# A graph attention kernel: Q by edge in SBUF two batches ahead, E in two PSUM banks one batch ahead, block sums in Q's bank, and gathers tied at every second batch

## The chip, the cores and the metric

The kernel runs on one core of one Trainium2 chip. Time is device time in microseconds (us) of one execution; the kernel before has a median of 2043.54 us over ten runs (2042.44 to 2047.0). The engines are TensorE (PE in the profile, PEld for its weight loads), VectorE (DVE), ScalarE (ACT), GpSimd (POOL) and SyncE (SP, whose queue issues most transfers).

## The reference

One layer of attention over a graph with 6250 nodes and 206250 directed edges, eight heads of 16 columns, followed by a residual and a layer norm:

```
Qh, Kh, Vh = h @ WQ, h @ WK, h @ WV            # 6250 x 128 each
Eh = edge_attr @ WE                            # 206250 x 128
score = exp(clip(sum_d(Kh[src] * Qh[dst] * Eh) / 4, -5, 5))     # per edge and head
msg = Vh[src] * score
h_out = segment_sum(msg, dst) / (segment_sum(score, dst) + 1e-6)
x = layernorm(x + h_out)
```

Edges come sorted by dst. src is random, so the rows of K and V must be gathered.

## The kernel before, in words

**Tiles and batches.** The edges are cut into 1612 tiles of 128. `cut_batches` joins four tiles into a batch of 512 edges (the last five batches are smaller), which gives 406 batches. The main loop at L481 runs once for each batch b, and four times more to drain.

**Tables.** At the start `table` (L226) computes K and V of every node and stores them to device memory as `kv` (1 KB a row). `q_rows` (L256) computes Q of 128 nodes, splits it into three bf16 parts and stores them as `qs`; `load_q` (L269) loads a window of 42 nodes (126 rows of parts) for eight tiles.

**Gathers.** `gather(b)` (L308) issues, for each tile of a batch, one indirect DMA on POOL (L315), which fetches 128 rows by `src` into a buffer of the pool "gather" with GB = 15 buffers. The first 12 batches (XB) fetch rows of x instead, and `project` (L326) makes K and V out of them on PE while the table is still being written. From batch 16 (LOCK) on, the first gather of every batch carries a manual dependency (L318 to L323), the tie: it waits for Q's matmul of batch b - lag(b). `lag` falls from 12 to STEP = 1 as b grows and stays at 1 from batch 60 on.

**The work of a batch**, spread over four iterations:

- `stage_0` (called two batches ahead, AHEAD = 2), on DVE: the one-hot matrix of edges by node, `onehot` (L343, f32), and its transposed form by Q's rows, `onehotT` (L347, bf16).
- `stage_a` (iteration b), on PE: Q by edge, `qps` (L357), copied to SBUF by ACT as `qT` (L359, two buffers); then E, `eps` (L361), which stays in PSUM.
- `pairs` (iteration b), on DVE: `eq` = qT times eps (L368).
- `turn` (iteration b + 1), on PE: four transposes of eq into `pps` (L376).
- `stage_b` (iteration b + 2), on DVE: `kq` = gathered K times pps (L382), the sum by head `sc` (L385), the clip (L388).
- `weigh` (iteration b + 2), on ACT: the two exponentials (L394, L396).
- `messages` (iteration b + 3), on DVE: `msg` = gathered V times weight (L423), the last use of the gather's buffer.
- `stage_c` (iteration b + 3), on PE: `agg` (L441), one-hot times messages, summed in PSUM for eleven tiles, copied by ACT (L454). `finish` (L407) joins such sums for two blocks of 128 nodes (`finps`), and `layernorm` follows in single steps that `fill` puts between other DVE instructions.

**Order of the work.** Each engine runs its instructions in the order in which they were issued. From iteration 12 on (`manual_schedule`, L483) that is the order written in the loop; before, Tile's scheduler may change it. In iteration b, PE runs turn(b-1), Q(b), E(b), then agg(b-3). DVE runs stage_b(b-2), messages(b-3), onehot and onehotT of b+2, then pairs(b). Other one-time work on DVE stands early: `from_window(1)` at batch 14 (L152 to L165), `relative` at batch 20 (L178), `count_inside` at batch 60 (L191 to L201).

**PSUM.** Eight banks: one for E (`psE`), one for Q (`psQ`), two for pps (`psP`), one (`psT`, tag "oT") for row blocks, projections' transposes, finishing sums and the count, two for agg (`psA`) and one (`psX`) that is always in use. The tables and the projections borrow from the first three through `pair_bank` (L218).

Of the kernel before, what the change touches and what calls it, by code (L numbers as in the profile page):

```python
# [8 lines left out]
F32 = mybir.dt.float32  # L9
I32 = mybir.dt.int32  # L10
BF16 = mybir.dt.bfloat16
# [13 lines left out]
MW = D + H  # L25
B = 4
CH = 8
GB = 15
XB = 12
LOCK = XB + 4  # L30
STEP = 1
TAIL = 8
HEAD = 132
NG = (NT + G - 1) // G
AHEAD = 2
EB = 6
SLAG = 2
WT = 8
# [42 lines left out]
def edge_attention(ctx: ExitStack, tc: tile.TileContext, x, xT, srcT, dstT, dstB, dst0, bnd, lo, eaT,  # L81
# [30 lines left out]
    with ExitStack() as fast:  # L112
# [78 lines left out]
        def count_inside():  # L191

            W = 4 * 2 * D
            for a in range(0, NT, W):
                e = min(NT, a + W)
                cl = wp.tile([P, W], F32, name="cl", tag="kvst", bufs=2)[:, :e - a]
                count(P, cl, rel[:, a:e], P - 1)
            nc.vector.tensor_reduce(cn[:, :1], cn, axis=AX.X, op=ALU.add)
            pc = psT.tile([1, 1], F32, name="pc", tag="oT")
            nc.tensor.matmul(pc, cn[:, :1], ones, start=True, stop=True)  # L200
            nc.vector.tensor_copy(cnt_i, pc)  # L201

# [1 line left out]
        ep = fast.enter_context(tc.tile_pool(name="edges", bufs=EB))  # L204
        wp = fast.enter_context(tc.tile_pool(name="work", bufs=3))
        sp = fast.enter_context(tc.tile_pool(name="sums", bufs=7))
        psE = fast.enter_context(tc.tile_pool(name="psE", bufs=1, space=bass.MemoryType.PSUM))
        psQ = fast.enter_context(tc.tile_pool(name="psQ", bufs=1, space=bass.MemoryType.PSUM))
        psP = fast.enter_context(tc.tile_pool(name="psP", bufs=2, space=bass.MemoryType.PSUM))
        psT = fast.enter_context(tc.tile_pool(name="psT", bufs=1, space=bass.MemoryType.PSUM))  # L210
        psA = fast.enter_context(tc.tile_pool(name="psA", bufs=2, space=bass.MemoryType.PSUM))
        psX = fast.enter_context(tc.tile_pool(name="psX", bufs=1, space=bass.MemoryType.PSUM))

# [3 lines left out]

        def pair_bank(i, name, shape):  # L218

            pool, tag = ((psE, "eps"), (psP, "pps"), (psQ, "qps"), (psP, "pps"))[i % 4]  # L220
            return pool.tile(shape, F32, name=name, tag=tag)


# [31 lines left out]

        def q_rows(q):  # L256
            n = min(P, N - q * P)
            ps = psT.tile([P, D], F32, name="qrows", tag="oT")
            nc.tensor.matmul(ps[:n], xT_sb[:, LEFT + q * P:LEFT + q * P + n], wq_sb, start=True, stop=True)
            st = wp.tile([P, QP, D], BF16, name="qst", bufs=1)  # L260
            r1 = wp.tile([P, D], F32, name="qr1", bufs=1)
            nc.scalar.copy(st[:n, 0, :], ps[:n])
            nc.vector.tensor_tensor(r1[:n], ps[:n], st[:n, 0, :], op=ALU.subtract)
            nc.scalar.copy(st[:n, 1, :], r1[:n])
            nc.vector.tensor_tensor(st[:n, 2, :], r1[:n], st[:n, 1, :], op=ALU.subtract)
            nc.sync.dma_start(qs[q * P * QP:(q * P + n) * QP].rearrange("(p s) f -> p s f", s=QP), st[:n])
            built.append(q)
# [17 lines left out]
            nc.sync.dma_start(rels[c][:, :n], relD.rearrange("j e -> (j e)")[None, c * RC * P:c * RC * P + n]  # L285
                              .to_broadcast([QROWS, n]))

        chunks, aggs, sums, pair_sums, st8, expanded = {}, {}, {}, {}, {}, {}

        def load_chunk(c):  # L290
            if c in chunks or c * CH >= NT:
# [16 lines left out]
        def gather(b, made=None):  # L308
            rows, f = (x, D) if b < XB else (kv, 2 * D)
            g = gp.tile([P, B, 2 * D], F32, name="kvrows")  # L310
            for i, t in enumerate(batches[b]):
                k = min(P, (E - t * P + 63) // 64 * 64)
                if k < P:
                    nc.vector.memset(g[k:, i, :], 0.0)
                ins = nc.gpsimd.indirect_dma_start(  # L315
                    out=g[:k, i, :f], out_offset=None, in_=rows,
                    in_offset=bass.IndirectOffsetOnAxis(ap=src_col(t)[:k], axis=0))
                if i == 0 and b >= LOCK:  # L318
                    made = expanded[b - lag(b)]
                if i == 0 and made is not None:  # L320
                    tc.add_manual_dep(ins.ins, made.ins.name,
                                      mybir.DependencyInfo(mybir.DependencyClass.Sync, mybir.DependencyReason.DATA),
                                      reason="gathers keep to TensorE's pace")  # L323
            return g

        def project(g, n):  # L326

            pt = psT.tile([P, B, P], F32, name="xtps", tag="oT")
            for i in range(n):
                nc.tensor.transpose(pt[:, i, :], g[:, i, :D], ident)  # L330
            xgT = wp.tile([P, B, P], F32, name="xgT", tag="kq", bufs=2)
            nc.scalar.copy(xgT[:, :n], pt[:, :n])
            for i in range(0, n, 2):
                k = min(2, n - i)
                pk = pair_bank(i // 2, "kvps", [P, 2, 2 * D])
                for j in range(k):
                    nc.tensor.matmul(pk[:, j, :], xgT[:, i + j, :], wkv_sb, start=True, stop=True)
                nc.scalar.copy(g[:, i:i + k, :], pk[:, :k, :])  # L338

        def stage_0(b):  # L340
            t0, n = batches[b][0], len(batches[b])
            oh = wp.tile([P, B, P], F32, name="onehot", bufs=AHEAD + 5)
            nc.vector.tensor_tensor(oh[:, :n], iota_p[:, None, :].to_broadcast([P, n, P]),  # L343
                                    rel[:, t0:t0 + n, None].to_broadcast([P, n, P]), op=ALU.is_equal)
            ohT = wp.tile([QROWS, B * P], BF16, name="onehotT", bufs=AHEAD + 2)
            e0 = t0 % RC * P
            nc.vector.tensor_scalar(ohT[:, :n * P], rels[t0 // RC][:, e0:e0 + n * P], node[:QROWS], None,  # L347
                                    op0=ALU.is_equal)
            st8[b] = oh, ohT

        def stage_a(b, g):
            t0, n = batches[b][0], len(batches[b])
            if b < XB:
                project(g, n)
            oh, ohT = st8.pop(b)
            pq = psQ.tile([P, B * P], F32, name="qps")
            expanded[b] = nc.tensor.matmul(pq[:, :n * P], loaded[t0 // WT], ohT[:, :n * P], start=True, stop=True)  # L357
            qT = wp.tile([P, B * P], F32, name="qT", bufs=2)
            nc.scalar.copy(qT[:, :n * P], pq[:, :n * P])  # L359
            pe = psE.tile([P, B * P], F32, name="eps")  # L360
            nc.tensor.matmul(pe[:, :n * P], we_sb, ea_tiles(t0, n), start=True, stop=True)  # L361
            st8[b] = [n, g, oh, pe, qT]

        def pairs(b):

            n, g, oh, pe, qT = st8[b]
            eq = wp.tile([P, B * P], F32, name="eq", bufs=2)
            nc.vector.tensor_tensor(eq[:, :n * P], qT[:, :n * P], pe[:, :n * P], op=ALU.mult)  # L368
            st8[b] = [n, g, oh, eq]

        def turn(b):

# [34 lines left out]
        def finish(j):  # L407

            q = 2 * j
            ps = psT.tile([P, 2, MW], F32, name="finps", tag="oT")  # L410
            for r in range(3):
                nc.tensor.matmul(ps, shift[:, P - OFF[r]:2 * P - OFF[r]], pair_sums[j][:, r], start=r == 0, stop=False)  # L412
            rest = [(i, (q + i + d, r), d * P + OFF[r]) for i in range(2) for d, r in ((-1, 2), (1, 0))]
            rest = [x for x in rest if x[1] in sums]
            for n, (i, k, s) in enumerate(rest):
                nc.tensor.matmul(ps[:, i], shift[:, P - s:2 * P - s], sums[k], start=False, stop=n == len(rest) - 1)
            fin = sp.tile([P, 2, MW], F32, name="fin", bufs=2)
            nc.scalar.copy(fin, ps)
            pending.append(layernorm(nc, sp, fin, xbs.pop(q), out, q, 2, stores))
# [55 lines left out]
        def fill():  # L475

            if norms and next(norms[0], None) is None:
                norms.pop(0)

        held = []  # L480
        for b in range(nbat + 4):  # L481
            if b >= XB and not manual:
# [5 lines left out]
            if b < nbat:  # L488
# [7 lines left out]
                    relative(C0, NT)  # L496
                if b == 14:
                    from_window(1)
                if b == 0:
                    for i in range(AHEAD):  # L500
                        stage_0(i)
                if b > 0:
                    turn(b - 1)
                stage_a(b, g)
            elif b == nbat:
                turn(b - 1)
            norms.extend(pending)
            pending.clear()
            for j in ready:
# [4 lines left out]
            if 0 <= b - 3 < nbat:  # L514
                messages(b - 3)
            fill()
            if b + AHEAD < nbat:
                stage_0(b + AHEAD)
            if b < nbat:
                pairs(b)  # L520
            if 0 <= b - 2 < nbat:
                weigh(b - 2)
            if 0 <= b - 3 < nbat:
                stage_c(b - 3)
            fill()
            if b < nbat:
                while len(built) < q_built(min(NJ - 1, batches[b][0] // WT + QLOOK + 2)):
                    q_rows(len(built))
# [162 lines left out]
```

## Time and profile before

| what | value |
|---|---|
| median of ten runs | 2043.54 us (2042.44 to 2047.0) |
| the profiled execution, its own time | 2044.03 us |
| its span in the trace | 2042.2 us |
| granted clock of TensorE, mean | 0.878 |
| busy: PE / DVE / ACT / POOL | 1431.8 / 1565.1 / 473.3 / 1533.8 us |
| gathers on POOL | 48 of x rows and 1564 of K and V rows, mean 951 ns |
| first and last gather's start | 3.60 and 2026.36 us |
| kq (L382): time that DVE waited for gathered rows | 348.7 us, 162 times |

The rest comes from one profiled execution. A row of a group gives line, engine and operation, what is written from what, the count, then busy time and mean ns, then the engine's idle time just before such instructions and what ended most of it. A row of the timeline gives start, duration, engine, line and operation, and in brackets the idle time before it. A row of the waits gives the total, the number of times and the longest, in us. Registers, semaphores and the issuing of a transfer on a queue are not counted as busy.

### The profile page before, as it was taken

Reading aid. Unit: us, or ns where it says so; the run is one execution under the profiler, and the core shown is the slowest. Engines: PE = TensorE matmul, PEld = TensorE weight load, DVE = VectorE, ACT = ScalarE, POOL = GpSimd, SP = SyncE. Lnnn points to the kernel's source line nnn. Section 1 sums busy time; section 2 is a strip of 40 time slices with the busy share of each in tenths; the row PEclk is TensorE's granted clock in tenths of the full one; section 3 lists DMA queues with packets and bytes.
Section 4 is the critical chain, followed back from the end, with each engine's and each line's share of the span. In section 5 each row is a group of like instructions: output and inputs, shape, how many; then the busy total and the mean of one; then the engine's idle time right before and its main releaser. Section 6 shows DMA issues by size and latency. Waiting matters only on the chain.

```text
span 2042.2 us, 24333 instructions
## 1 busy us (share of the span) xinstructions
PE 1431.8 (70%) x6736; PEld 992.2 (49%) x6736; DVE 1565.1 (77%) x3542; ACT 473.3 (23%) x1548; POOL 1533.8 (75%) x1619
## 2 busy tenths in 40 slices
PE   6977876776776667666767667776766676666765
PEld 4655554454544445444454444444544444444544
DVE  3689998777777778677787777776877777777776
ACT  2422222221222222222222222221222222222221
POOL 7777777777777777777777777777777777777775
PEclk9989998888889888889788888888888888888888
DMA  9777766656666676666665676667565666666652
GB/s 300 225 230 204 221 200 207 192 173 217 186 198 183 187 209 175 203 174 200 201 188 175 197 204 198 185 186 214 171 203 172 201 208 180 195 178 203 202 170 82
DMA packets 177711, 398.12 MB, mean 195 GB/s; under 512 B 60988, under 2 KB 86758, under 8 KB 177568
## 3 DMA queue, kind: packets, MB, share of 16 engines
q0 software_dynamic: 76592, 208.18, 34.8%
q1 hardware_dynamic: 99836, 187.38, 29.6%
q8 instruction: 56, 0.92, 0.2%
q10 hardware_dynamic: 1140, 0.93, 0.2%
q14 instruction: 87, 0.71, 0.1%
HBM read 381.54 MB, written 14.81 MB: 194 GB/s over the span
## 4 chain that ended last, share of the span: by engine, by line
DMA 33%; DVE 28%; POOL 17%; issue 12%; PE 8%; ACT 1%; DVEq 0%; SPq 0%; POOLq 0%; ACTq 0%
DMA kvrows<-kv,src 32%; POOL kvrows L315 17%; DVE kq L382 7%; DVE sc L385 7%; DVE msg L423 3%; DVE eq L368 3%; DVE onehot L343 3%; PE agg L441 3%; PE eps L361 2%; DVE onehotT L347 2%; DVE sc L388 1%; PE pps L376 1%; DMA kv<-kvst 1%; PE qps L357 1%; PE finps L412 0%
## 5 line engine op out<-in xcount | busy, mean ns | idle before, releaser
L315 POOL DMA_INDIRECT kvrows<-kv,src x1564 | 1487.2, 951 | 476.5 <-issue 362.0
L441 PE MATMUL agg<-msg,onehot 128*128 128x136 f32 x3224 | 530.9, 314 | 512.8 <-DVE msg L423 410.5
L441 PEld LDWEIGHTS agg<-msg,onehot 128*128 128x128 f32 x3224 | 470.5, 215 | 833.1 <-issue 666.6
L382 DVE TENSOR_TENSOR kq<-kvrows,pps 128x512 f32<-128x512 f32 x406 | 275.6, 679 | 351.2 <-DMA kvrows<-kv,src 348.7
L361 PE MATMUL eps<-ea,we_sb 128*128 128x512 f32 (+1 forms) x812 | 478.5, 674 | 0.7 <-ACT kvrows L338 0.7
L359 ACT COPY qT<-qps 128x512 f32<-128x512 f32 x406 | 236.3, 582 | 544.5 <-PE qps L357 542.8
L376 PE MATMUL pps<-shift,eq 128*128 128x128 f32 x1612 | 302.2, 317 | 62.9 <-DVE eq L368 59.5
L368 DVE TENSOR_TENSOR eq<-qT,eps 128x512 f32<-128x512 f32 x406 | 273.3, 673 | 20.7 <-PE eps L361 16.7
L385 DVE TENSOR_REDUCE sc<-kq 128x32 f32<-128x512 f32 x406 | 276.1, 680 | 8.9
L423 DVE TENSOR_TENSOR msg<-kvrows,bank 128x512 f32<-128x512 f32 x406 | 274.4, 676 | 5.5 <-ACT bank L394 5.4
L343 DVE TENSOR_TENSOR onehot<-bank,dst_sb 128x512 f32<-128x512 f32 x406 | 274.9, 678 | 0.0
L394 ACT ACTIVATE bank<-sc 128x32 f32<-128x32 f32 x406 | 81.8, 201 | 823.8 <-DVE onehot L343 812.3
L376 PEld LDWEIGHTS pps<-shift,eq 128*128 128x128 f32 x1612 | 208.0, 160 | 120.8 <-DVE eq L368 114.8
L361 PEld LDWEIGHTS eps<-ea,we_sb 128*128 128x128 f32 x812 | 180.5, 224 | 29.8 <-ACT kvrows L338 3.7
L357 PE MATMUL qps<-onehotT,qw 126*128 126x512 bf16 x406 | 177.9, 438 | 0.7 <-ACT qT L359 0.7
L347 DVE TENSOR_SCALAR onehotT<-relb,node 126x512 bf16<-126x512 bf16 x406 | 154.7, 382 | 6.0 <-DMA relb<-relD 5.2
L388 DVE TENSOR_SCALAR sc<-sc 128x32 f32<-128x32 f32 x406 | 90.1, 222 | 9.0
L396 ACT ACTIVATE msg<-sc 128x32 f32<-128x32 f32 x406 | 86.5, 213 | 0.2
L315 POOL DMA_INDIRECT kvrows<-x,src x48 | 45.6, 951 | 16.4 <-issue 12.2
L454 ACT COPY sum<-agg 128x136 f32<-128x136 f32 x146 | 38.6, 264 | 33.1 <-PE agg L441 31.4
L357 PEld LDWEIGHTS <-qw 126*128 126x128 bf16 x406 | 45.1, 111 | 1.1 <-issue 1.0
L412 PE MATMUL finps<-sum,shift 128*128 128x272 f32 x144 | 37.4, 397 | 0.0
(69 smaller groups left out, 465.5 us busy)
## 6 DMA issues: line engine op xcount, KB each, us to landing
ea<-eaT SPq DMA_DIRECT2D x201, 512.0 KB
relb<-relD SPq DMA_DIRECT2D x100, 504.0 KB
kvrows<-kv,src POOLq DMA_INDIRECT x1564
qw<-qs SPq DMA_DIRECT2D x202, 31.5 KB
kv<-kvst SPq DMA_DIRECT2D x12, 512.0 KB
qs<-qst SPq DMA_DIRECT2D x48, 96.0 KB
xb<-x SPq DMA_DIRECT2D x24, 128.0 KB
out<-h SPq DMA_DIRECT2D x24, 128.0 KB
```

The lines of the kernel that those rows point to most:

```text
L315: ins = nc.gpsimd.indirect_dma_start(out=g[:k, i, :f], out_offset=None, in_=rows, in_offset=bass.IndirectOffsetOnAxis(ap=src_col(t)[:k], a ...
L343: nc.vector.tensor_tensor(oh[:, :n], iota_p[:, None, :].to_broadcast([P, n, P]), rel[:, t0:t0 + n, None].to_broadcast([P, n, P]), op=ALU.i ...
L347: nc.vector.tensor_scalar(ohT[:, :n * P], rels[t0 // RC][:, e0:e0 + n * P], node[:QROWS], None, op0=ALU.is_equal)
L357: expanded[b] = nc.tensor.matmul(pq[:, :n * P], loaded[t0 // WT], ohT[:, :n * P], start=True, stop=True)
L359: nc.scalar.copy(qT[:, :n * P], pq[:, :n * P])
L361: nc.tensor.matmul(pe[:, :n * P], we_sb, ea_tiles(t0, n), start=True, stop=True)
L368: nc.vector.tensor_tensor(eq[:, :n * P], qT[:, :n * P], pe[:, :n * P], op=ALU.mult)
L376: nc.tensor.transpose(pp[:, i, :], eq[:, i * P:i * P + P], ident)
L382: nc.vector.tensor_tensor(t1[:, :n], g[:, :n, :D], pp[:, :n], op=ALU.mult)
L385: nc.vector.tensor_reduce(sc[:, :n], t1[:, :n].rearrange("p b (h d) -> p b h d", h=H), axis=AX.X, op=ALU.add)
L423: nc.vector.tensor_tensor(m[:, :n, :D].rearrange("p b (h d) -> p b h d", h=H), g[:, :n, D:].rearrange("p b (h d) -> p b h d", h=H), exp_p[ ...
L441: nc.tensor.matmul(aggs[k], oh[:, i, :], m[:, i, :], start=first and not final, stop=last)
```

## The change

Three constants change: GB from 15 to 14, STEP from 1 to 0, and AHEAD is replaced by QA = 2 and EA = 1. `stage_0` and `stage_a` are cut into four functions.

- Q's matmul and its copy to SBUF (`expand_q`) run two batches ahead, at the end of the iteration, behind agg; `qT` gets four buffers, and `onehotT` three.
- E's matmul (`expand_e`) runs one batch ahead, into one of two banks, at Q's former place behind the transposes of `turn`.
- `onehotT` is still built two batches ahead, now ahead of the other; `onehot` is built in iteration b itself, just before `pairs`.
- Row blocks, projections' transposes, finishing sums and the count go to Q's bank; the bank `psT` is gone, and its place is E's second.
- The tie names E's matmul of batch b - lag(b), where lag now falls to 0 (at batch 64), and only even batches have it.
- Before the loop, onehotT and Q of batches 0 and 1 and E of batch 0 are issued.

```diff
-GB = 15
+GB = 14
-STEP = 1
+STEP = 0
-AHEAD = 2
+QA = 2
+EA = 1
...
-            pc = psT.tile([1, 1], F32, name="pc", tag="oT")
+            pc = psQ.tile([1, 1], F32, name="pc", tag="qps")
...
-        psE = fast.enter_context(tc.tile_pool(name="psE", bufs=1, space=bass.MemoryType.PSUM))
+        psE = fast.enter_context(tc.tile_pool(name="psE", bufs=2, space=bass.MemoryType.PSUM))
-        psT = fast.enter_context(tc.tile_pool(name="psT", bufs=1, space=bass.MemoryType.PSUM))
...
-            pool, tag = ((psE, "eps"), (psP, "pps"), (psQ, "qps"), (psP, "pps"))[i % 4]
+            pool, tag = ((psE, "eps"), (psP, "pps"))[i % 2]
...
-                if i == 0 and b >= LOCK:
+                if i == 0 and b >= LOCK and b % 2 == 0:
                     made = expanded[b - lag(b)]
...
-            pt = psT.tile([P, B, P], F32, name="xtps", tag="oT")
+            pt = psQ.tile([P, B, P], F32, name="xtps", tag="qps")
...
+        def one_hot(b):
+            t0, n = batches[b][0], len(batches[b])
+            hot[b] = wp.tile([P, B, P], F32, name="onehot", bufs=6)
+            nc.vector.tensor_tensor(hot[b][:, :n], iota_p[:, None, :].to_broadcast([P, n, P]),
                                     rel[:, t0:t0 + n, None].to_broadcast([P, n, P]), op=ALU.is_equal)
+        def one_hot_rows(b):
+            hotT[b] = wp.tile([QROWS, B * P], BF16, name="onehotT", bufs=3)
...
+        def expand_q(b):
+            pq = psQ.tile([P, B * P], F32, name="qps")
+            nc.tensor.matmul(pq[:, :n * P], loaded[t0 // WT], hotT.pop(b)[:, :n * P], start=True, stop=True)
+            qTs[b] = wp.tile([P, B * P], F32, name="qT", bufs=QA + 2)
+            nc.scalar.copy(qTs[b][:, :n * P], pq[:, :n * P])
+        def expand_e(b):
+            pes[b] = psE.tile([P, B * P], F32, name="eps")
+            expanded[b] = nc.tensor.matmul(pes[b][:, :n * P], we_sb, ea_tiles(t0, n), start=True, stop=True)
+        def pairs(b, g):
+            eq = wp.tile([P, B * P], F32, name="eq", bufs=3)
+            nc.vector.tensor_tensor(eq[:, :n * P], qTs.pop(b)[:, :n * P], pes.pop(b)[:, :n * P], op=ALU.mult)
...
+        for b in range(QA):
+            one_hot_rows(b)
+            expand_q(b)
+        for b in range(EA):
+            expand_e(b)
...
-                if b > 0:
-                    turn(b - 1)
-                stage_a(b, g)
-            elif b == nbat:
+            if 0 < b <= nbat:
                 turn(b - 1)
+            if b < nbat and b < XB:
+                project(g, len(batches[b]))
+            if b + EA < nbat:
+                expand_e(b + EA)
...
-            if b + AHEAD < nbat:
-                stage_0(b + AHEAD)
+            if b + QA < nbat:
+                one_hot_rows(b + QA)
             if b < nbat:
-                pairs(b)
+                one_hot(b)
+                pairs(b, g)
...
             fill()
+            if b + QA < nbat:
+                expand_q(b + QA)
```

## The prediction

> **What bounds the kernel now.** I read the busy shares first, then who waits for whom, then single instructions in order of time. The busy shares alone mislead: VectorE (DVE) is busiest, and the chain that ended last is put down to DMA and DVE.
>
> ```profile
> PE 1431.8 (70%) x6736; PEld 992.2 (49%) x6736; DVE 1565.1 (77%) x3542; ACT 473.3 (23%) x1548; POOL 1533.8 (75%) x1619
> POOL 7777777777777777777777777777777777777775
> DMA 33%; DVE 28%; POOL 17%; issue 12%; PE 8%; ACT 1%; DVEq 0%; SPq 0%; POOLq 0%; ACTq 0%
> L315 POOL DMA_INDIRECT kvrows<-kv,src x1564 | 1487.2, 951 | 476.5 <-issue 362.0
> L382 DVE TENSOR_TENSOR kq<-kvrows,pps 128x512 f32<-128x512 f32 x406 | 275.6, 679 | 351.2 <-DMA kvrows<-kv,src 348.7
> ```
>
> POOL stands at 7 tenths in every slice but the last: that evenness is the clue. Its idle time before gathers, 476.5 us over 1564, is 0.305 us each. The waits of POOL show that no pause before a gather is longer, whatever is named as releaser:
>
> ```profile
> POOL kvrows L315 <- issue: 374.1, 1228, 0.3
> POOL kvrows L315 <- DVE sc L388: 19.2, 63, 0.3
> POOL kvrows L315 <- DVE kq L382: 14.0, 46, 0.3
> POOL kvrows L315 <- PE eps L361: 13.7, 45, 0.3
> ```
>
> In all 1612 rows of POOL's timeline the pause is 0.29 to 0.32 us, on first gathers of a batch (which carry the tie) and on the others alike (the first of all, which waited for its indices, apart). So neither tie nor buffer ever held POOL: it issues a gather each 0.95 + 0.30 = 1.25 us, without a hole, from 3.60 to 2026.36 us. 1611 steps of 1.2505 are 2014.6; the other 8.8 us are gathers that took longer (69 of them above 0.965 us). After the last gather's start come 15.8 us of tail to the span's 2042.2. DVE's 348.7 us for kq are DVE waiting for POOL's rows: it does a batch in some 3.6 us when rows are there (kq to kq, shortest 3.58), POOL gives one each 5.0.
>
> **What the change must do to matter.** Time moves only if POOL stops, a gather gets longer, or the tail moves. I take the edits by these three.
>
> *Ties.* A gather's first piece waits now for Q's matmul of batch b-1; then for E's matmul of batch b, at even b only. Removing half the ties frees 0 us, as tied gathers show the same 0.30. Both matmuls stand in iteration b-1 behind the same transposes, so the new one ends later by E instead of Q: 1.02 less 0.38 at full clock, up to 1.9 less 0.4 at a low one, so 0.6 to 1.5 us. From batch 60 on, the time from Q's copy (L359, the row that Q's matmul releases) to the gather has median 6.7 us and the smallest are 0.93 (batch 62), 1.08 (405), 1.12 (181), 1.38 (285), 2.12 (404). Three of the four below 1.5 are odd and lose their tie. Batch 62 stays tied: there PE waited 4.98 us for the count at L198, and E ran 1.9 us at a low clock. Its stall is 0 to 0.6; I take **+0.4**. While the lag is longer than that (batches 16 to 60), the new tie names work one iteration earlier than before, so it is looser.
>
> *GB 15 to 14.* A gather's buffer is free once msg (L423) of batch b-14 is done, not b-15. In steady state that is at least 49 us back. Early it is not: gathers start at 3.6, the first kq runs at 59.32, and by batch 25 the lead has shrunk. msg of batch 11 ends at 124.06 (held by the count and the window at L152 to L165), the gather of batch 25 starts at 129.31: 5.2 us, the smallest; batches 14 to 24 have 9 or more. Nothing is lost unless the first batches come over 5.2 us later: **0**.
>
> *PSUM banks early.* Row blocks, first projections and the finishing sums move from a bank of their own into Q's. In written order Q(0) and Q(1) now stand before the first projection's transposes. Today these run at 40.76, Q(0) at 54.15 (its qw loads are issued at 49.22) and Q(1)'s copy ends at 56.69. If the bank keeps that order, projection 0 starts at 56.7 and needs 0.66 + 0.58 + 2 x 1.0 + 0.58 and some 0.5 of hand-overs, to 61.0: 1.7 us after 59.32. As PE is 12.9 of 15 us busy from 55 to 70, and 18.0 of 18 from 90 to 108, the three transposes and the projection done earlier today (3 x 0.65 + 2.07 = 4.0) may come on top instead: 1.7 to 4.0 us, below the 5.2. If the bank goes to whoever is ready, it is 0. Cover gone, it costs the excess over 5.2; that is the main rival.
>
> *E a batch ahead in two banks, Q two ahead in SBUF.* The numbers of matmuls (812 and 406), copies (406 x 582 ns) and products stay. What goes is DVE's wait for PE before eq (16.7 us) and PE's and ACT's mutual waits; all of it lies beside the 1.25 us beat, so 0. Next late after it is again the gathered rows. SP's loads of qw now serve a matmul two iterations sooner: issued six batches ahead, they keep four, 20 us. The Q matmul now stands behind agg (L441), which waits for msg; it has two iterations until eq needs it.
>
> *The longer gathers.* Which DVE row lies across them? Of the 69, 47 overlap onehotT (L347), against 362 of the 1543 others. One of them:
>
> ```profile
> 435.12 0.34 DVE L347 TENSOR_SCALAR onehotT<-relb,node 126x512 bf16<-126x512 bf16 x1
> 435.22 1.05 POOL L315 DMA_INDIRECT kvrows<-kv,src  x1 [0.30 <-issue]
> ```
>
> It is a matter of phase: onehotT lengthens a gather (0.03 to 0.11 us) when it starts 0.22 to 0.07 us before it, and hardly otherwise. 43 hits cost 3.3 us today. The change puts onehotT ahead of onehot, 0.60 us earlier (L343's start to L347's). Moving every L347 row by 0.50 to 0.70 us against POOL's beat gives 19 to 82 hits, 1.2 to 5.9 us; at 0.60 it is 25 and 2.0. That leaves -2.1 to +2.6, and I take **0**, near the -1.3 of the 0.60, because the beat itself slides after each hit. The 1.5 us at 145.5 (L178) and 1.1 at 309 to 312 (L147) stay.
>
> The Trainium skill, page "SBUF — State Buffer", section "SBUF: two separate sides", says that VectorE in its two-port modes and GpSimd lock each other out for a whole instruction. Taken alone it would let every one of those overlaps hold a gather, some 0.34 x 406 = 138 us (an estimate from it), in both kernels alike, and the move would cost nothing; the 362 overlapped gathers of ordinary length say that only a short part of a gather can be held, so the phase rule above stands.
>
> *Tail.* From 2019.2 on DVE has no pause. Today the one-hots of the last batches are built two iterations ahead; then they are built in their own, so two of 256 columns (0.33 us start to start) move into this stretch: **+0.7**. The work after the last agg (2032.4) stays.
>
> Sum: 0.4 + 0 + 0 + 0 + 0.7 = +1.1 on the profiled execution's own 2044.03 (span 2042.2), so 2045.1. The median of the ten runs is 0.5 below that execution, so I predict **2044.6**; by the terms' ends, 2041.4 (-2.1) to 2047.7 (+0.6 + 0.9 + 2.6).
>
> **Rivals.**
> - *Slower: the early lead is used up.* Place: gathers of batches 25 to 30, waiting for msg 14 batches back. Price: the delay of the first 12 batches less 5.2 us, never made up, as POOL has no slack. If each of the 12 projections shows both copies that now take turns in one bank (2 x 0.58 + 2 x 0.2 = 1.56), the delay is 4.0 + 18.7 = 22.7 and the loss 17.5: 2062. With a third of it 10.2 and 5.0: 2049.6. It decides (over 4.1 in all) from a delay of about 8.2. For: PE is full there. Against: PE already runs other batches' matmuls between these copies today (transposes, Q, agg at 89 to 92 us). 0.13.
> - *Slower by the small terms together* (phase, ties, tail at their upper ends and a little of the lead): 2048. 0.03.
> - *Faster: nearly all lengthening of gathers goes.* At most 8.8 us; without the 2.6 of L178 and L147, 6.2: 2038. It needs layer-norm rows (L624 lies across the 1.18 at 870.2 and 1450.5) to move out of phase too. 0.06.
> - *The change does nothing*, as no tie bound anything: 2043.5. It lies inside the forecast.
>
> Forecast 0.78, with its own range 2041.4 to 2047.7, all of it no change. Something like 0.2% (4 us) is what a measurement of this kernel can tell from nothing. Faster 0.06, within 0.78, slower 0.16. The range for 8 in 10 goes a little way into the slow rival: 2041 to 2050.
>
> **What would show it.** Right: POOL at 7 in every slice, pauses before L315 still at most 0.32 (one of some 0.7 near 317 us), kq's wait for rows near 350 us, the eq wait on PE gone, last gather near 2026. Wrong: a pause of a us or more on POOL at 125 to 155 us (early lead), pauses on even batches later (ties), or many more gathers above 0.965 us (phase).

## The result and the profile after

The changed kernel takes 2051.59 us (median of 8 runs, 2051.11 to 2053.36), the kernel before, run beside it, 2044.28 us (28 runs, 2041.97 to 2048.82). The ratio is 1.0037, with a 95% interval of 1.0028 to 1.0046: the change costs 7.3 us, where no change was forecast. The ratios here and below leave out executions that took over 1.5% longer than the fastest of the same kernel: one each of `rows_early`, `pf_re` and `rows_early_c`, and four of the six of `rows_early_d`.

On the page of the changed kernel, POOL's slices are as even as before. The groups show line, engine, operation, busy time and mean ns, then the idle time before:

```profile
PE 1447.4 (70%) x6736; PEld 962.7 (47%) x6736; DVE 1559.5 (76%) x3542; ACT 468.1 (23%) x1548; POOL 1537.0 (75%) x1619
L315 POOL DMA_INDIRECT kvrows<-kv,src x1564 | 1490.2, 953 | 483.4 <-issue 381.3
L385 DVE TENSOR_TENSOR kq<-kvrows,pps 128x512 f32<-128x512 f32 x406 | 275.4, 678 | 318.9 <-DMA kvrows<-kv,src 300.1
L371 DVE TENSOR_TENSOR eq<-qT,eps 128x512 f32<-128x512 f32 x406 | 272.7, 672 | 4.5 <-PE eps L365 4.3
L259 PE MATMUL qrows<-wq_sb,xT_sb 128*128 128x128 f32 (+1 forms) x98 | 26.9, 361 | 32.7 <-ACT qT L359 30.5
L263 DVE TENSOR_TENSOR qr<-qrows,qst 128x128 f32<-128x128 f32 (+1 forms) x49 | 14.3, 292 | 77.6 <-ACT qst L262 77.6
```

The wait of eq for PE is nearly gone (4.3 us, 16.7 before), and DVE's wait for gathered rows is shorter (300.1, 348.7 before). New are the last two rows, the row blocks of Q: PE now waits 30.5 us ahead of them for ACT's copy of Q out of the same bank (0.7 us in all before), and DVE stands still in them for 77.6 us. In the waits of the kernel before that was:

```profile
DVE qr L263 <- ACT qst L262: 16.2, 39, 1.7
```

The time itself is lost on POOL. Of its waits for other engines one alone has a longest entry over 0.3 us (the columns are total, times and longest); its timeline has the places. No other pause is over 0.57 us, the first gather's wait for its indices apart.

```profile
POOL kvrows L315 <- PE eps L365: 9.0, 9, 4.0
```

```profile
145.00 1.92 PE L365 MATMUL eps<-ea,we_sb 128*128 128x512 f32 x2
147.19 0.94 POOL L315 DMA_INDIRECT kvrows<-kv,src  x1 [2.93 <-PE eps L365]
148.70 0.95 POOL L315 DMA_INDIRECT kvrows<-kv,src  x1 [0.57 <-issue]
...
332.64 1.02 PE L365 MATMUL eps<-ea,we_sb 128*128 128x512 f32 x2
333.94 0.95 POOL L315 DMA_INDIRECT kvrows<-kv,src  x1 [3.96 <-PE eps L365]
```

The two held gathers are the first of batch 28 and the first of batch 64, both tied. Each starts 0.27 us after the matmul that its tie names has ended: E of batch 19 at 146.92, E of batch 64 at 333.66. In the kernel before, the same two places look so:

```profile
142.56 0.38 PE L357 MATMUL qps<-onehotT,qw 126*128 126x512 bf16 x1
144.29 0.95 POOL L315 DMA_INDIRECT kvrows<-kv,src  x1 [0.30 <-issue]
...
323.82 0.38 PE L357 MATMUL qps<-onehotT,qw 126*128 126x512 bf16 x1
327.70 0.94 POOL L315 DMA_INDIRECT kvrows<-kv,src  x1 [0.30 <-PE pps L376]
```

Q of batch 19 was done 1.35 us before batch 28's gather, Q of batch 63 3.5 us before batch 64's. Those were the margins, less the 0.27 us of hand-over from a tied matmul's end to its gather's start.

**The sum.** Over the usual 0.30, the three pauses cost 2.63 + 0.27 + 3.66 = 6.56 us. From the last gather's start to the end it is 17.47 us, 15.84 before: +1.63. Gathers that took over 0.965 us lost 7.8 us against the ordinary ones, 8.8 before: -1.0. Together 7.2 us; the medians differ by 7.3. (The profiled execution took 2055.84, 4.3 over its median: its step from gather to gather was 1.2530 us where four variants of it have 1.2499 to 1.2502. That belongs to this execution, not to the change.)

**Theory:** batches run late from the start on, and the tie, whose margin was 1.35 us, passes that on to POOL. **Rivals:** the fourteenth buffer; the thinning of the ties in itself; the count at batch 60 alone.

### The profile page after: what moved, and what is told of

Same layout as the page of the kernel before. It is cut to its first block, busy times and chain, and to the rows that moved or that the text cites. A ratio compares the mean times of both kernels' runs of the same rounds, so it can differ in the third digit from the quotient of the medians.

```text
span 2054.0 us, 24090 instructions
## 1 busy us (share of the span) xinstructions
PE 1447.4 (70%) x6736; PEld 962.7 (47%) x6736; DVE 1559.5 (76%) x3542; ACT 468.1 (23%) x1548; POOL 1537.0 (75%) x1619
## 4 chain that ended last, share of the span: by engine, by line
DMA 29%; DVE 28%; POOL 17%; issue 12%; PE 10%; ACT 2%; DVEq 0%; SPq 0%; POOLq 0%; ACTq 0%
DMA kvrows<-kv,src 27%; POOL kvrows L315 17%; DVE kq L385 7%; DVE sc L388 6%; PE agg L444 4%; DVE msg L426 3%; DVE onehot L343 3%; DVE eq L371 3%; DVE onehotT L350 2%; DVE sc L391 1%; PE eps L365 1%; ACT qT L359 1%; PE qrows L259 1%; PE kvps L337 1%; DMA kv<-kvst 1%
## 5 line engine op out<-in xcount | busy, mean ns | idle before, releaser
L444 PE MATMUL agg<-msg,onehot 128*128 128x136 f32 x3224 | 543.4, 318 | 523.5 <-DVE msg L426 427.3
L444 PEld LDWEIGHTS agg<-msg,onehot 128*128 128x128 f32 x3224 | 479.7, 218 | 842.9 <-issue 682.0
L385 DVE TENSOR_TENSOR kq<-kvrows,pps 128x512 f32<-128x512 f32 x406 | 275.4, 678 | 318.9 <-DMA kvrows<-kv,src 300.1
L365 PE MATMUL eps<-ea,we_sb 128*128 128x512 f32 (+1 forms) x812 | 484.4, 683 | 0.0
L379 PEld LDWEIGHTS pps<-shift,eq 128*128 128x128 f32 x1612 | 223.4, 164 | 119.9 <-DVE eq L371 89.5
L365 PEld LDWEIGHTS eps<-ea,we_sb 128*128 128x128 f32 x812 | 148.8, 227 | 0.7
L263 DVE TENSOR_TENSOR qr<-qrows,qst 128x128 f32<-128x128 f32 (+1 forms) x49 | 14.3, 292 | 77.6 <-ACT qst L262 77.6
L259 PE MATMUL qrows<-wq_sb,xT_sb 128*128 128x128 f32 (+1 forms) x98 | 26.9, 361 | 32.7 <-ACT qT L359 30.5
```

Of the source, the lines that this page charges most:

```text
L365: expanded[b] = nc.tensor.matmul(pes[b][:, :n * P], we_sb, ea_tiles(t0, n), start=True, stop=True)
L379: nc.tensor.transpose(pp[:, i, :], eq[:, i * P:i * P + P], ident)
L385: nc.vector.tensor_tensor(t1[:, :n], g[:, :n, :D], pp[:, :n], op=ALU.mult)
L444: nc.tensor.matmul(aggs[k], oh[:, i, :], m[:, i, :], start=first and not final, stop=last)
```

## The experiments

The first comparison and the first four kernels ran where the kernel before takes 2044 us ("the first chip" below, though the comparison may have run on another of its kind). The later ones ran on four other chips, on which it takes 2407 to 2434 us. Each ratio is to the kernel before on the same chip.

### Which wait holds POOL

`no_ties`: the tie's condition is never true.

```diff
-                if i == 0 and b >= LOCK and b % 2 == 0:
+                if i == 0 and b >= NT:
```

> The changed kernel without any tie. Theory A (the tie names work that the late start of the first batches has not yet reached: pauses of POOL of 2.6 us at batch 28 and 3.7 us at batch 64): both pauses go, POOL's pause is 0.30 everywhere, and the time falls by 6 to 7 us, to within 0.1% of the kernel before (tail +1 to +2 us). Theory B (the early lead is used up through the 14 buffers): the wait for msg of batch b-14 takes over around batches 25 to 28, with pauses of 2 us or more there, and the time falls by less than 3 us. Theory C (a longer beat of the gathers, 1.2530 instead of 1.2502 us, comes with the change): the time falls by 6 us at most and stays 0.2% above the kernel before, with a beat of 1.253.

2045.23 us, ratio 1.0003 [0.9994, 1.0012]. No pause is left in its waits of POOL:

```profile
POOL kvrows L315 <- issue: 392.4, 1288, 0.3
POOL kvrows L315 <- PE eps L365: 0.3, 1, 0.3
```

The smallest margin to the buffer (gather of batch 25 after msg of batch 11) was 1.5 us there, with 14 buffers. So the ties cost the time, not the buffer. E of batch 19 was done 1.3 us after batch 28's gather there, which no longer cared.

`step_1`: STEP = 1, so the lag never falls to 0.

```diff
-STEP = 0
+STEP = 1
```

> The changed kernel with the lag's floor at 1 again. Theory A: the pause at batch 64 (the first with lag 0) goes, the one at batch 28 stays: 3 to 4 us less than the changed kernel, still 0.15 to 0.2% above the kernel before. Theory B: no change, since the buffers decide. Theory C: no change.

2048.22, 1.0017 [1.0008, 1.0025]. The pause at 64 is gone, the one at 28 stays. Timeline of its POOL:

```profile
133.07 0.95 POOL L315 DMA_INDIRECT kvrows<-kv,src  x1 [2.82 <-DVE onehotT L350]
...
150.71 0.95 POOL L315 DMA_INDIRECT kvrows<-kv,src  x1 [2.93 <-PE eps L365]
```

The upper row is a third kind: the untied gather of batch 25. msg of batch 11 ended at 132.80 in this execution (first kq at 67.0, not 65.55), so here the buffer held it; the releaser named merely starts then. This held gather started 0.27 us after that end; in the changed kernel the same gather started 0.27 us after its buffer too, with the usual pause of 0.30: there was nothing to spare. The rival I gave most weight to was that close.

### Where the delay comes from

`project_first`: Q of batches 0 and 1 and E of batch 0 are issued behind the first projection.

```diff
-        for b in range(QA):
-            one_hot_rows(b)
-            expand_q(b)
-        for b in range(EA):
-            expand_e(b)
...
+            if b == 0:
+                for i in range(QA):
+                    expand_q(i)
+                for i in range(EA):
+                    expand_e(i)
```

(The two `one_hot_rows` stay ahead of the loop.)

> The changed kernel, with Q of batches 0 and 1 and E of batch 0 issued in iteration 0 behind the first projection, so that the first transposes get Q's bank first. Theory A, with the bank's order as the cause of the late start: kq of batch 0 returns from 65.5 to about 60 us, msg of batch 11 from 129.3 to 124 to 126, the pause at batch 28 goes and that at batch 64 shrinks by as much as the start moves: 3 to 6.5 us less than the changed kernel. If the taking of turns in the bank during all 12 projections is the cause and not the start, kq of batch 0 comes earlier but msg of batch 11 stays near 129 and the time falls by less than 2 us.

In the trace the first kq comes at 62.9 (65.5 in the changed kernel, 59.3 before), the pause at 28 is gone and the one at 64 (3.96) is alone. So 2.6 of the 6.2 us of late start are the place of Q(0), Q(1) and E(0). The times don't follow: this execution took 2048.66, but the median of five is 2052.61 (up to 2053.95), 1.0036 [1.0023, 1.0049]. What the others lost is not settled; on the time, the expectation failed.

`own_bank`: row blocks, projections, finishing sums and the count have a bank of their own again; E has one bank and is made in its own iteration (EA = 0); STEP = 1.

```diff
-STEP = 0
+STEP = 1
-EA = 1
+EA = 0
...
-        psE = fast.enter_context(tc.tile_pool(name="psE", bufs=2, space=bass.MemoryType.PSUM))
+        psE = fast.enter_context(tc.tile_pool(name="psE", bufs=1, space=bass.MemoryType.PSUM))
+        psT = fast.enter_context(tc.tile_pool(name="psT", bufs=1, space=bass.MemoryType.PSUM))
...
-            ps = psQ.tile([P, D], F32, name="qrows", tag="qps")
+            ps = psT.tile([P, D], F32, name="qrows", tag="oT")
```

(The other three tiles likewise.)

> The changed kernel with one bank for E, E made in its own iteration, and the bank psT back for transposes, row blocks, finishing sums and the count; lag's floor at 1; Q by edge still two batches ahead, ties still at even batches, 14 buffers. Theory A with the shared bank as cause: kq of batch 0 near 59 to 60 us, DVE's wait for the row blocks' copy (77.6 us in all) back near 16, no pause of POOL over 0.5 us, time within 0.1% of the kernel before. Theory B: pauses at batches 25 to 28 stay. If the lead is lost to Q's place at the end of the iteration and not to the bank, the pauses stay too.

2048.19, 1.0017 [1.0008, 1.0025]. Its start is as late (first kq at 65.5), as the loads of Q's windows are issued at 56.9 instead of 49.2 (48.2 in the changed kernel), and it too pauses at 28 (2.42), with shorter pauses (0.43 to 0.99) at 12, 20, 26 and 40. So the expected start, the absence of pauses and the 0.1% did not come. But it catches up: kq of batch 60 is 4.1 us later than before, 8.8 in the changed kernel, and DVE's wait in the row blocks is half:

```profile
DVE qr L264 <- ACT qst L263: 39.7, 47, 4.6
```

### On chips where PE's results come late

POOL's pauses make the time there too, but they are far more: 138 to 185 over 0.33 us in a trace, 361 to 641 us in all in the table below. Behind them stand stops of the other engines. In every trace from these chips PE, DVE and ACT stand still together some 100 times, for 1.5 to 13 us; POOL goes on until a tie or a full buffer holds it. One such place, in `before_even` (ACT's timeline; its source was the matmul at 1192.34, 0.38 us long):

```profile
1192.34 0.38 PE L357 MATMUL qps<-onehotT,qw 126*128 126x512 bf16 x1
```

```profile
1203.48 0.58 ACT L359 COPY qT<-qps 128x512 f32<-128x512 f32 x1 [12.10 <-remote]
1203.96 0.21 ACT L394 ACTIVATE bank<-sc 128x32 f32<-128x32 f32 x1
1204.09 0.22 ACT L396 ACTIVATE msg<-sc 128x32 f32<-128x32 f32 x1
1204.21 0.26 ACT L454 COPY sum<-agg 128x136 f32<-128x136 f32 x1
```

"remote" says that the profile finds no event on this core that released it. The first to go on is nearly always an instruction that takes a result of PE (of qps, eps, agg, finps, qrows or pps). In the trace's record of semaphores, what comes just before it is an update of PE's own in 90 of 93 stops (`tie_all_b`), 107 of 110 (`before_even`) and 124 of 124 (`before_no_ties`). The single instructions of ACT and POOL are as long as elsewhere (copy 0.58, gather 0.95 us).

Seven edits take up what the first chip had left open: `rows_early` (row blocks ahead of weighing and aggregation, four times, the later ones `_b`, `_c`, `_d`), `gb_15`, `count_late`, `tie_all`, `before_even`, `pf_re` (`project_first` and `rows_early`) and the last without ties; and, for the ties themselves, `before_no_ties`.

```diff
                 one_hot(b)
                 pairs(b, g)
+            if b < nbat:
+                while len(built) < q_built(min(NJ - 1, batches[b][0] // WT + QLOOK + 2)):
+                    q_rows(len(built))
             if 0 <= b - 2 < nbat:
                 weigh(b - 2)
...
                 expand_q(b + QA)
-            if b < nbat:
-                while len(built) < q_built(min(NJ - 1, batches[b][0] // WT + QLOOK + 2)):
-                    q_rows(len(built))
...
-GB = 14
+GB = 15
...
-            qTs[b] = wp.tile([P, B * P], F32, name="qT", bufs=QA + 2)
+            qTs[b] = wp.tile([P, B * P], F32, name="qT", bufs=QA + 1)
...
-            eq = wp.tile([P, B * P], F32, name="eq", bufs=3)
+            eq = wp.tile([P, B * P], F32, name="eq", bufs=2)
...
-            if b == min(60, nbat):
+            if b == min(100, nbat):
...
-            if b == min(80, nbat + 1):
+            if b == min(120, nbat + 1):
...
-                if i == 0 and b >= LOCK and b % 2 == 0:
+                if i == 0 and b >= LOCK:
```

In that order: `rows_early`, `gb_15` (three rows), `count_late` (the count, and the reading of its result), `tie_all`. `before_even` adds `and b % 2 == 0` to the kernel before, `before_no_ties` has `b >= NT` there.

> The changed kernel, with the row blocks of Q (L256) issued ahead of weigh and agg instead of behind Q's matmul at the end of the iteration; they stay in Q's bank. Theory A2 (the early loss of lead is kept up because DVE waits 1.4 us for each row block, 77.6 us in all, behind msg, agg, Q and Q's copy): that wait falls to 15 to 25 us, the lag of kq behind the gathers at batch 60 falls from 13.7 us to 6 to 9, the pause at batch 64 goes or shrinks to under 1 us, the one at batch 28 loses up to 1.4 us: 3.5 to 5 us less than the changed kernel. Rival (only the late start counts): kq's lag at batch 60 changes by under 2 us, and the time by under 2 us.

> The changed kernel with 15 gather buffers again; for the room, qT has three buffers and eq two. Theory A (ties, not buffers, make the pauses): both pauses stay, time within 0.1% of the changed kernel. Theory B (buffers): 2 us or more less. In runs with a start later than the profiled one, the wait for msg of batch 11 (0.3 us from binding, and 2.8 us long in the run with lag 1) goes with the fifteenth buffer, so a gain of 1 to 2 us on the median stays possible under A.

> The changed kernel with the count at batch 100 instead of 60. Theory A3 (the pause at batch 64 needs the count's 6 us on DVE just ahead of the first lag of 0): the pause at 64 goes or is under 0.5 us, and none over 1 us comes at batch 102 to 104, since the lag is worked off by then: 3 to 4 us less than the changed kernel. Rival (lag 0 alone does it): a pause of 2 us or more stays at 64, and one may come at 104.

> The changed kernel with the tie at every batch. Theory A (the pause is set by how far the work is behind the tie's batch, so a pause at an even batch serves the odd one after it): pauses of POOL of 6 to 8 us in all, time within 0.1% of the changed kernel. Rival (leaving out every second tie is what keeps the cost down): pauses at odd batches add 2 us or more.

On this chip (before 2433.7): 1.0588 [1.0543, 1.0634], 1.0710 [1.0672, 1.0748], 1.0728 [1.0702, 1.0754] and 1.0068 [1.0048, 1.0087]. The expected numbers were for a kernel before of 2044 us, so none of the theories is decided here. What comes out: with ties at even batches alone it is 6 to 7% slower, with all ties 0.7%.

> The changed kernel with the row blocks of Q issued ahead of a batch's weighing and aggregation, as they stand free of them before the change, so that DVE need not wait through them for Q's copy. If the pause of 3.96 us at batch 64 stands because the late start is caught up too slowly, and that because DVE waits 77.6 us in the row blocks: those waits fall below 40 us, the lag at batch 60 falls from 13.7 to about 8, the pause at 64 goes or falls under 1 us, the one at 28 (3.5 in all) stays: 2047.5 to 2048.5. Rival: the count alone makes batch 64 late, whatever the lag: pause near 4, 2051.6.

> The kernel before, with its tie at even batches only and nothing else changed. If a tie costs only where the compute side is behind at the tied batch: before has no pause over 0.32 us, and this has none either: 2044.3, within 1 us. Rival, that thinning the ties costs something by itself (gathers that run up to a batch further ahead, then are held longer): pauses of over 1 us at even batches, 2047 or more.

> The changed kernel, all its ties kept, with both delays taken away: Q of batches 0 and 1 and E of batch 0 are issued behind the first projection, and the row blocks of Q ahead of weighing and aggregation. If late start and slow catch-up make the two pauses: none over 1 us at batches 28 and 64, last gather near 2027, and what stays is the tail (1.65): 2045.5 to 2046.5. Rival, the tie to E's matmul is late in itself: at least one pause of 3 to 4 us stays, 2048 to 2052.

> The changed kernel with its tie (to E's matmul) at every batch in place of every second. If what decides is how far the compute side is behind: the same 6.5 us of pauses, spread over neighbours of batches 28 and 64, 2051 to 2052.5. Rival, that it is the thinning that costs: the pauses go or fall below 2 us in all, 2046 to 2047.

Before 2407.4: 1.0331 [1.0312, 1.0351], 1.0804 [1.0783, 1.0824], 1.0310 [1.0263, 1.0358] and 0.9998 [0.9977, 1.0018]. `before_even` differs from the kernel before in the ties alone. Here thinning them costs 8% by itself. That was the second rival; on the first chip `no_ties` speaks against it, as there the changed kernel without any tie is within 0.1% of the kernel before, but `before_even` did not run there. With all ties the rest of the change costs nothing that can be measured on this chip, and 0.7% on the one above.

> The changed kernel with the row blocks of Q issued ahead of weighing and aggregation. On a chip where the kernel before takes about 2044 us: if the pause of 3.96 us at batch 64 comes of a catch-up slowed by DVE's waits in the row blocks, those waits (77.6 us) fall below 40, the pause at 64 goes or falls under 1 us, the one at 28 stays: 2047.5 to 2048.5. Rival, that the count alone makes batch 64 late: pause near 4, 2051.6. On a chip where it takes 2400 or more: 3 to 6% above it, as before.

> The kernel before with its tie at even batches only. Where PE has no stalls of its own (the kernel before at 2044): no pause over 0.32 us and 2044.3, within 1 us, since no tie of it ever bound. Where PE stalls (before at 2400 or more): 8% above it, as measured once. Rival, that thinning costs by itself: 2047 or more where before takes 2044.

> The changed kernel, ties kept, first projection ahead of Q of batches 0 and 1, and row blocks ahead of weighing. Where before takes 2044: no pause over 1 us if late start and catch-up are the causes, 2045.5 to 2046.5; rival, the tie to E's matmul is late in itself: a pause of 3 to 4 us stays, 2048 to 2052. Where before takes 2400 or more: 3% above it.

> As the last, with no ties. Where before takes 2044: nothing holds the gathers but their buffers, 2045 to 2046 (tail 1.65 longer, phase 0.9 shorter), so not better than before. Where PE stalls (before at 2400 or more): by the theory that a tie held too long is what costs there, below the ratio of every tied version, 1.00 or less; by the rival, that gathers without ties disturb PE, above 1.03.

Before 2407.7: 1.0345 [1.0305, 1.0385], 1.0799 [1.0775, 1.0823], 1.0300 [1.0267, 1.0333] and 1.0971 [1.0946, 1.0995]. So the ties are not what makes the time longer on these chips: without them it is worse.

> The changed kernel with the row blocks of Q ahead of weighing and aggregation. Where the kernel before takes 2044: DVE's waits in row blocks below 40 us, the pause at 64 gone or under 1 us if the slow catch-up makes it, 2047.5 to 2048.5; rival, the count alone: pause near 4, 2051.6. Where it takes 2400 or more: 3.3% above it, as three times before.

> The kernel before without any tie. Where it takes 2044 with its ties: no tie ever bound, so 2044.3, within 1 us. Where it takes 2400 or more: if the time follows the number of ties whatever the rest (all 1.00, every second 1.08), 1.08 to 1.11, with PE's stalls longer (650 us or more in all); if it is the rest of the change, 1.00 to 1.02.

Before 2408.9: 1.0258 [1.0208, 1.0308] and 1.1278 [1.1253, 1.1303]; the second lies above the 1.08 to 1.11 expected. In the kernel before: all ties 1, every second 1.08, none 1.13. The page of `before_no_ties` shows where ACT waits, above that of `tie_all_b`:

```profile
L359 ACT COPY qT<-qps 128x512 f32<-128x512 f32 x406 | 236.1, 582 | 1388.7 <-remote 842.0
```

```profile
L359 ACT COPY qT<-qps 128x512 f32<-128x512 f32 x406 | 237.0, 584 | 786.1 <-remote 474.7
```

The table adds up, from 200 us on, the times over 1.5 us in which PE, DVE and ACT all stand, and in the whole trace what POOL's pauses have over 0.30 us, the first gather's apart:

| kernel | ties | us | these stops | POOL's pauses | ratio to before |
|---|---|---|---|---|---|
| `tie_all_b` | all | 2405 | 93, 308 us | 361 us | 0.9998 |
| `rows_early_b` | every second | 2485 | 105, 440 us | 437 us | 1.0331 |
| `before_even` | every second | 2600 | 110, 533 us | 548 us | 1.0804 |
| `pf_re_noties` | none | 2644 | 118, 694 us | 572 us | 1.0971 |
| `before_no_ties` | none | 2716 | 124, 644 us | 641 us | 1.1278 |

POOL's pauses account for the time: the spans of the first three are 362, 438 and 547 us longer than the 2042.2 of the kernel before on the first chip; in the last two, whose gathers run ahead of the other engines as far as the buffers let them, the stretch after the last gather's start is 50 and 52 us instead of 16 as well. So ties that never held POOL on the first chip do hold it here, and without ties full buffers do. In the waits of POOL, `before_even` above `before_no_ties`:

```profile
POOL kvrows L315 <- PE qps L357: 495.2, 89, 10.6
```

```profile
POOL kvrows L315 <- DVE msg L423: 587.3, 116, 7.6
```

With fewer ties the stops get more, by up to a third, and above all longer: 3.3 us each in `tie_all_b`, 5.2 to 5.9 without ties. On the first chip the kernel before has 30 of them, 88 us, and all end with gathered rows. Why PE's results come late on the other chips, and why fewer ties make that worse, is open. In the place shown above, the transfers' share of the DMA engines is 1.05 from 1194 to 1199 us, 0.79 from 1199 to 1203 and 0 from 1203 on, just before ACT goes on; whether PE's results wait for transfers no run tests. Row blocks issued early are the one other edit that seems to help there: `rows_early` is, by the ratios, 1.1 and 1.3% below `gb_15` and `count_late` on one chip. The changed kernel itself did not run there.

## Why the prediction was wrong

- **POOL as the bound: right.** Where no tie holds, gathers follow each other by 1.2499 to 1.2502 us (1.2530 in the profiled execution of the changed kernel), and the loss is POOL's pauses plus the tail.
- **The step that failed: "While the lag is longer than that (batches 16 to 60), the new tie names work one iteration earlier than before, so it is looser", and with it +0.4 for the ties; measured, they cost 6.6 us.** Looser it is: the iteration gained is worth 4.1 us at batch 28 (transposes at 137.96 and 142.10 in the kernel before), and E in place of Q takes 1.9 of it, as E ran at a granted clock of 0.52 and ended 2.8 us after the transposes' start where Q ended 0.8 after its own. What failed is that the delay of the early batches was never held against a tie. I had read the margins from batch 60 on only; the early ones were in the trace of before, the smallest 1.35 us at batch 28. The delay there was 6.2 us (the transposes ahead of E(19) at 144.15, that iteration's at 137.96 before). PE in the kernel before, then in the changed one:

```profile
137.96 1.11 PE L376 MATMUL pps<-shift,eq 128*128 128x128 f32 x4 [0.20 <-DVE eq L368]
142.10 0.62 PE L376 MATMUL pps<-shift,eq 128*128 128x128 f32 x4
```

```profile
144.15 1.06 PE L379 MATMUL pps<-shift,eq 128*128 128x128 f32 x4
```

6.19 + 2.77 - 0.84 - 4.14 = 3.98: E(19) ended 4.0 us after Q(19) had, and 4.0 - 1.35 is the pause of 2.6 (the 0.27 of hand-over and the 0.27 by which POOL was late already cancel). At batch 64, the first with lag 0 (not 62, as I had it: there the tie still names E(61), an iteration back), the delay was 8.8 us, and E takes 0.6 longer than Q, against a margin of 3.5 and 2.6 by which POOL was late already: 3.3, and with 0.3 of hand-over the pause. The medians go the same way: 2051.59, 2048.22 without the pause at 64 (`step_1`), 2045.23 without either (`no_ties`); that of `project_first`, whose trace has no pause at 28, does not (2052.61).
- **The delay was too small by more than half**: 1.7 to 4.0 predicted, 6.2 at the first kq, 5.2 at the end of msg of batch 11, 8.8 at batch 60. And it was held only against the buffer's 5.2 us of slack, not against the tie's 1.35. I had looked for it in Q's bank. But projection 0 was done at 59.26 (61.0 predicted), and the transposes that the first kq reads at 60.15. What the first kq then waited for is DVE's order: eq of batch 2 stands ahead of it, and waits for E(2), which PE runs behind the projection of batch 1.

```profile
59.55 0.60 PE L379 MATMUL pps<-shift,eq 128*128 128x128 f32 x4
63.55 1.02 PE L365 MATMUL eps<-ea,we_sb 128*128 128x512 f32 x2
64.68 0.69 DVE L371 TENSOR_TENSOR eq<-qT,eps 128x512 f32<-128x512 f32 x1 [4.13 <-PE eps L365]
65.55 0.68 DVE L385 TENSOR_TENSOR kq<-kvrows,pps 128x512 f32<-128x512 f32 x1
```

In the kernel before the first kq stands ahead of eq of batch 1. The loop as written has kq(0) ahead of eq(2) too; before iteration 12 Tile's scheduler may change it. The same wait is 3.25 us in `project_first`, nearly all that was left of the delay there. This is read from the traces; no run takes that order away.
- **A wait that I had not listed**: Q's bank is one bank, and its users take turns in written order. A row block of Q stands behind agg and Q's copy (PE waits 30.5 us for that copy), and DVE in turn behind the row block's: 77.6 us for 16.2. `own_bank` halves that and catches up 4.7 us more by batch 60, though it changes E's place too. On chips with late PE results, `rows_early` took a further part away (91.1 us, 223 to 239 in the three others there). For the pause at 64 on the first chip this is argued, not shown: `rows_early` did not run on such a chip, nor did `count_late`, so the count's share (5.2 us of PE waiting at batch 60) stays open.
- **GB 14 at 0: right, but only just**: the gather of batch 25 started 0.27 us after its buffer, as a held one does; in `step_1`, with a later start, it cost 2.5 (2.82 less 0.30). What it costs in the executions that were not profiled is open, as `gb_15` did not run on such a chip. My main rival, buffers at batches 25 to 30, named the right batches and the wrong wait.
- **E and Q ahead at 0: right in the steady state, not at the start.** The 16.7 us of eq are gone and buy nothing; of the 4.3 left, 4.13 are the one wait ahead of the first kq.
- **onehotT's phase at 0, within -2.1 to +2.6: right**, -1.0. The Trainium skill, page "SBUF — State Buffer", section "SBUF: two separate sides", lets whichever of VectorE (in a two-port mode) and GpSimd starts first hold the other off for its whole instruction, so the estimate of 138 us, in which every overlap holds a gather, asked too much of it. In the changed kernel, as before, about 70 of 1612 gathers are longer at all (71, 69 before). The overlap shows on DVE too: in the kernel before, an onehotT that starts 0.45 to 0.70 us into a gather takes up to 0.58 us instead of 0.34, and one that starts earlier into it takes 0.34. So of a gather's 0.95 us only a part holds DVE off.
- **The tail: +0.7 predicted, +1.63 measured** (+1.4 in `no_ties`). Not taken apart.

## What to carry to other kernels

A dependency that never bound has a margin, and it is the smallest margin anywhere that counts: list it for every tied batch, the early ones first, and hold every delay of the change against the smallest. A bank that is shared makes its users wait for each other in written order, so list what each new neighbour waits for. And a tie that costs nothing on one chip can be what keeps another fast: on the first chip no tie of the kernel before ever held POOL, and the changed kernel lost nothing without any; on the others the ties hold POOL for hundreds of us, and the kernel before with half of them is 8% slower.

## What the runs showed of the hardware

- On four of the chips one and the same kernel takes 2407 to 2434 us instead of 2044. Its mean granted clock there is 0.81 to 0.83 in all executions but one (0.73), and 0.88 to 0.90 on the chip of the first four kernels; but instructions at full clock last as long (two matmuls of E 1.02 us on both). The kernel before was not traced there. In the traces of its variants the difference is POOL's pauses, behind stops that end when a result of PE comes, 10.8 us after the matmul's recorded end in the place shown.
- In that place the granted clock is 0.50 from 1199 to 1206 us and 1.00 from 1208 on, and the two matmuls of E take 1.89 us at 1206.17 and 1.02 at 1209.63 (`before_even`). That agrees with the Trainium skill, page "TensorE: Matmul & The Clock Gate", section "What's actually happening": after an idle window of some 3.4 us the array runs at half its clock, and at full clock after a busy one. The lower clock follows the stop here; what makes the stops, no row shows.
- A single execution can have a longer step: 1.2530 us from gather to gather against 1.2502, gathers 949 against 946 ns and ACT's copies 586 against 585 ns (medians); over 1611 steps that is 4.5 us. The profiled executions of `count_late` and `pf_re_noties` have the longer step too.
